# Gathers of adjacency rows moved from the column search to layer 0 of a four-layer graph network

## The chip, the cores and the metric

The program runs on one core of one Trainium2 chip. The metric is the device time of one execution in microseconds (us), median of several runs; smaller is better. An engine is called by its short name: PE (TensorE, matmuls), DVE (VectorE), ACT (ScalarE), POOL (GpSimd) and SP (SyncE, which here only issues DMAs). Each engine runs its own instructions in order and waits on semaphores for the others.

## What is computed

Four layers of a graph network on 2708 nodes with 512 features. The adjacency matrix `adj` (2708 x 2708, float32) is sparse, with a diagonal that is never zero; the low-numbered nodes have most of the edges. After each layer the result is added to the input and normalised over the features.

```python
# layer 0
adj_hat = adj + eye
d = 1 / sqrt(adj_hat.sum(axis=1))
x = layernorm(x + ((d[:, None] * adj_hat * d[None, :]) @ x) @ W.T + b)
# layer 1
head = (adj > 0) / max(sqrt(sum over the row of (adj > 0)), eps)
inc = adj + head
x = layernorm(x + (inc @ x) / inc.sum(axis=1))
# layer 2: attention over the edges, and a second sum with adj
x = layernorm(x + sigmoid(attn_a * x_a + attn_b * x_b))
# layer 3
x = layernorm(x + relu(adj @ ((x > 0) @ sign(weight).T)))
```

## The kernel before

The 2708 nodes are cut into 22 blocks of 128 rows (the last has 20). Block b of a layer's output needs only those columns of `adj` in which one of its rows has an entry. The kernel first finds these columns, then works with packed tiles alone: `packed[b]` holds, for block b, tiles of 128 found columns each (128 x 128 numbers, 64 KB). `ROOM[b]` is the number of such tiles, 9 for block 1 falling to 1 for block 21, 107 in all. Block 0, which has almost all columns, is not searched: it keeps whole column blocks in `packed[0]`. `DIRECT` names column blocks that a block loads whole instead of by index; those go over SP. `GROUPS` joins the blocks into nine groups: 1; 2, 3; 4 to 6; 7 to 9; 10 to 12; 13 to 15; 16 to 18; 19, 20; 21.

**The search** (inside `with in_order()`, L1128) takes one block per turn. SP loads the block's rows of `adj` (1.35 MB, two halves, four buffers), its rows of x and a tile for block 0, two turns ahead. DVE turns the rows into a 0/1 mask (L782, L784), PE counts with it which columns are hit (L801), and PE also transposes the block's x (L943) and multiplies it with the layer's weights (L958); ACT sums the rows (L733), keeps the transposed x (L950) and scales the product by `dinv`, which gives y (L967), written to the table `y_rows` in DRAM (L968). For each group, in the turns after its last block, DVE, PE and ACT turn the hits into a list of column numbers: `count` and `count_partitions` in the first turn, `steps_of` and `look_up` (L849, L870) in the second, `keep_looked` and `list_nodes` (L880, L890 to L910) in the third. `list_nodes` ends with `row_at`, the indices for the adjacency gathers, and puts each gather of the group into the list `to_fetch`. From the end of that turn on, `fetch` issues up to six of them in each turn on POOL (L928): an indirect DMA that takes 128 rows of the transposed matrix, 512 bytes of each, into one tile of `packed[b]`. `in_order` fixes the order on every engine as it is written, but POOL has no other work in the search, so its gathers run as soon as their indices are there. `own_diagonal` (L810) and `fold` (L979) are small DVE steps of each turn. `count_block0` and block 0's y (L967, last) end the stage.

**Layer 0** (loop at L1237) goes over the blocks in the order of `sequence`: 0, 1, 21, 2, 3, up to 20. For each block, POOL gathers rows of `y_rows` by the found column numbers (L570, 128 rows of 2 KB, 256 KB), `ROOM[b]` gathers per block into tiles with 10 buffers; a gather has to wait until PE has used the tile of ten gathers before. PE multiplies each with the packed tile (L1254), DVE adds and normalises (L1264, L615 to L631), SP writes the result to `x1_rows` (L1268). A first gather of `y_rows` can't start before all 22 blocks of y are written. Between the blocks stand steps of other kinds, keyed by the place in the sequence (`between`): loads and sums for later layers, and for each group `count_positive`, which counts positive entries in its packed tiles (L1017 on DVE, L1019 on PE), and `head_steps`, which turn these counts into layer 1's factors (`head_row`, `rdeg`, `own1`). Group n has its counts after place 2 + 2n and the rest after place 3 + 2n.

**Layer 1** gathers rows of `x1_rows`, so its first gather waits for the last block's write. Layers 1 to 3 read the packed tiles from SBUF again and gather features in the same way. A dense version of the whole network stands behind a test and isn't run with these inputs.

Of the kernel before, what the change touches and what calls it, by code (L numbers as in the profile page):

```python
# [12 lines left out]
I32 = mybir.dt.int32  # L13
# [6 lines left out]
P = 128  # L20
# [465 lines left out]
def sparse_layers(ctx, tc, x, adj, adj_t, w0_t, b0, w_sa, a_sa, w_gcnb, b_gcnb, wa, ba, wb, bb, w3_t,  # L486
# [10 lines left out]
    nc = tc.nc  # L497
    N, D = x.shape
    KC = D // P
    NB = -(-N // P)  # L500
# [6 lines left out]
    def direct(b: int):  # L507

        return tuple(range(NB)) if b == 0 else DIRECT.get(b, ())
# [49 lines left out]
    own1 = const.tile([P, NB], F32, name="s_own1")  # L559
    head0_row = const.tile([P, P], F32, name="s_head0_row")  # L560
    vl_row = const.tile([P, D], F32, name="s_vl_row")
    for t in (*f, f0_other):
        nc.vector.memset(t[:, D + 1 :], 0.0)

# [85 lines left out]
    with tc.tile_pool(name="s_pre", bufs=1) as pre:  # L650
# [232 lines left out]
        def list_nodes(g):  # L883
            b0_ = g[0]
            T = sum(ROOM[b] for b in g)
            look = search.pop(g)["look"]
            own = small.tile([P, TS], F32, tag="turns", name=f"turns{b0_}")
            at = 0
            for b in g:
                nc.vector.tensor_tensor(  # L890
                    own[:, at : at + ROOM[b]], order[:, : ROOM[b]],
                    look[:, at : at + ROOM[b], NB], op=ALU.subtract,
                )
                at += ROOM[b]
            nc.vector.tensor_tensor(own[:, :T], own[:, :T], look[:, :T, NB + 1], op=ALU.subtract)
            col = look[:, :T, :NB]
            nc.vector.tensor_tensor(
                col, col, own[:, :T, None].to_broadcast([P, T, NB]), op=ALU.is_equal
            )
            nc.vector.tensor_tensor(  # L900
                col, col, start[:, None, :].to_broadcast([P, T, NB]), op=ALU.mult
            )
            nc.vector.tensor_reduce(own[:, :T, None], col, axis=AX.X, op=ALU.add)
            nc.vector.scalar_tensor_tensor(
                index_of[b0_][:, :T], own[:, :T], float(PAD), look[:, :T, NB + 2],
                op0=ALU.add, op1=ALU.add,
            )

            row_at = small.tile([P, TS], I32, tag="row_at", name=f"row_at{b0_}")
            nc.vector.tensor_scalar(  # L910
                row_at[:, :T], index_of[b0_][:, :T], N - 1, None, op0=ALU.min
            )
            at = 0
            for b in g:
                m = rows(b)
                for i, j in enumerate(direct(b)):
                    nc.sync.dma_start(
                        packed[b][:, i, :], adj_t[j * P : (j + 1) * P, b * P : b * P + m]
                    )
                for t in range(ROOM[b]):  # L920
                    to_fetch.append((b, t, row_at[:, at + t : at + t + 1]))
                at += ROOM[b]

        to_fetch = []

        def fetch(n: int):
            for b, t, row in to_fetch[:n]:
                nc.gpsimd.indirect_dma_start(  # L928
                    out=packed[b][:, t + len(direct(b)), :], out_offset=None, in_=adj_t,
                    in_offset=bass.IndirectOffsetOnAxis(ap=row, axis=0), element_offset=b * P,  # L930
                )
            del to_fetch[:n]

        sum0 = ps_mm.tile([P, D], F32, tag="sum0", name="l0_0", bufs=1)
        summed = []
# [160 lines left out]
        def turn(at: int):  # L1096
            step_of = {at - last_at[g]: g for g in GROUPS}

            def chain(action, since: int):
                if since in step_of:  # L1100
                    action(step_of[since])

            each(degree, at - 1)
            each(root, at - 1)
            each(lambda b: b and own_diagonal(b), at - 1)
            each(sum_rows, at)
            each(lambda b: b and mark(b), at)
            each(load_x, at + 2)
            each(load, at + 2)
            each(transpose_x, at)  # L1110
            chain(steps_of, 2)
            chain(count, 1)
            each(scale0, at - 2)
            each(keep_transposed, at)
            each(project0, at - 1)
            chain(keep_looked, 3)
            chain(count_partitions, 1)
            chain(look_up, 2)
            each(inverse_root, at - 1)
            each(fold, at - 3)  # L1120
            each(grow0, at - 3)
            chain(list_nodes, 3)
            if to_fetch:
                fetch(6 if at < NTURN else len(to_fetch))
            if at == NTURN:
                count_block0()

# [30 lines left out]
    with tc.tile_pool(name="s_l0", bufs=10, reuse_waits="tile") as lp:  # L1158
# [62 lines left out]
        def several(*actions):  # L1221
            def act():
                for a in actions:
                    a()
            return act
# [4 lines left out]
        several(*others)()  # L1230
        for n, g in enumerate(GROUPS):
            steps_ = head_steps(g)
            between.setdefault(2 + 2 * n, []).append(
                several(lambda g=g: count_positive(g, lp), steps_[0])
            )
            between.setdefault(3 + 2 * n, []).append(several(*steps_[1:]))
        for at, b in enumerate(sequence):  # L1237
            m = rows(b)
            if b:
                src = [  # L1240
                    gathered(lp, D, y_rows, b, t) for t in range(ROOM[b])
                ]
                dsrc = []
                for i, j in enumerate(direct(b)):
                    if j == b:
                        own = lp.tile([P, D], F32, tag="own", name=f"y_own{b}", bufs=1)
                        nc.sync.dma_start(own[:m], y_rows[b * P : b * P + m, :])
                        dsrc.append(own)
                    else:
                        dsrc.append(first[0])  # L1250
                src = dsrc + src
                ps = ps_mm.tile([P, D], F32, tag="mm", name=f"l0_{b}")
                for i, moving in enumerate(src):
                    nc.tensor.matmul(  # L1254
                        ps[:m], packed[b][:, i, :], moving[:, :D],
                        start=(i == 0), stop=(i == len(src) - 1),
                    )
            else:
                ps = sum0
            if at > 1:  # L1260
                grow1(sequence[at - 2])
            t = work.tile([P, D], F32, tag="t", name=f"t0_{b}")
            old = place_of_x(b)
            nc.vector.scalar_tensor_tensor(  # L1264
                t[:m], ps[:m], dinv[:m, b : b + 1], old[:m, :D], op0=ALU.mult, op1=ALU.add
            )
            layernorm(old[:m, :D], t, m, f"0_{b}")
            nc.sync.dma_start(x1_rows[b * P : b * P + m, :], old[:m, :D])  # L1268
            for step_ in between.get(at, []):
                step_()  # L1270
        for b in sequence[-2:]:
            grow1(b)
    l0_ps.close()
# [550 lines left out]
```

## Time and profile before

| what | us |
|---|---|
| median of 3 runs | 1210.41 |
| lowest and highest run | 1210.06, 1212.56 |
| the profiled execution, its own time | 1219.48 |
| its span, first to last instruction | 1217.8 |

| stage of the profiled execution | from | to | length |
|---|---|---|---|
| search, up to the first gather of `y_rows` | 0 | 239.2 | 239.2 |
| layer 0, up to the first gather of `x1_rows` | 239.2 | 415.3 | 176.1 |
| layer 1 | 415.3 | 575 | 159.7 |
| layer 2 | 575 | 1062 | 487 |
| layer 3 | 1062 | 1217.8 | 155.8 |

| POOL's gathers by line | number | busy us | mean ns |
|---|---|---|---|
| L928, adjacency rows | 107 | 110.2 | 1030 |
| L570, rows of `y_rows` | 107 | 105.6 | 987 |
| L570, rows of `x1_rows` | 107 | 113.0 | 1056 |
| L1492, layer 2's rows | 107 | 106.1 | 991 |
| L570, rows of `xw_rows` | 83 | 82.9 | 998 |

How to read the views: a row of the timeline has the start, the duration, the engine, the line of the program, the operation, the tile written and the tiles read, how many rows are merged, and in square brackets the idle time of that engine before it and what ended that. "issue" there means that the engine waited for nothing that the profile shows, and "remote" that the semaphore's move can't be tied to an instruction. In a table of windows each engine has its busy time in the stretch, and the last three columns are the granted share of PE's full clock, the busy share of the DMA engines and what they moved. Ends of matmuls are modelled, so their rows are surer in their start.

### The profile page before, as it was taken

The numbers are of one execution on the slowest core, as the hardware profiler recorded it, in microseconds if no ns is written. First come the engines' busy times: TensorE is split into PE (matmuls) and PEld (weight loads), VectorE is DVE, ScalarE is ACT, GpSimd is POOL, SyncE is SP. The second block draws the span as 40 slices with busy tenths as digits, with TensorE's granted clock in tenths as the row PEclk, the third lists the DMA queues.
The fourth block names the chain that finished last, engine by engine and source line by source line (L and its number), as shares of the span: only waits on it lengthen the run. The fifth ranks groups of instructions, "written<-read, shape, count | busy, mean of one in ns | idle before, by whom it ended". The sixth has DMA issues, their size and how long they took to land. (4 is left out here: it accounts for less than half of the span.)

```text
span 1217.8 us, 13502 instructions
## 1 busy us (share of the span) xinstructions
PE 1007.9 (83%) x4009; PEld 608.2 (50%) x4028; DVE 726.2 (60%) x2556; ACT 403.4 (33%) x869; POOL 533.5 (44%) x545
## 2 busy tenths in 40 slices
PE   3865677579789789989799999999999999698852
PEld 2432333123334234445566677676666666476631
DVE  4764556464567676778656655656555554346765
ACT  4542444100000044668533223223232322243420
POOL 0455544676666377675332233222221211066660
PEclk9877778789799899999899999999999999889976
DMA  9875775476677677776332223223121211199982
GB/s 330 297 230 182 222 228 157 113 243 200 199 201 224 188 202 207 216 218 205 87 84 75 66 74 97 65 57 88 51 85 40 79 40 53 57 338 287 256 238 80
DMA packets 84523, 193.53 MB, mean 159 GB/s; under 512 B 13680, under 2 KB 26968, under 8 KB 84440
## 3 DMA queue, kind: packets, MB, share of 16 engines
q0 software_dynamic: 41056, 113.12, 33.8%
q1 hardware_dynamic: 31692, 64.45, 15.5%
q10 hardware_dynamic: 11692, 15.01, 3.8%
q8 instruction: 34, 0.56, 0.2%
q14 instruction: 49, 0.40, 0.1%
HBM read 155.73 MB, written 25.92 MB: 149 GB/s over the span
## 5 line engine op out<-in xcount | busy, mean ns | idle before, releaser
L1492 POOL DMA_INDIRECT xg<-x_rows,i x107 | 106.1, 991 | 216.9 <-DVE mv L619 63.3
L1337 PE MATMUL acc<-ae,xg 128*128 128x256 f32 x856 | 187.9, 378 | 0.4 <-ACT ae L1330 0.3
L1337 PEld LDWEIGHTS acc<-ae,xg 128*128 128x128 f32 x856 | 161.9, 190 | 23.0 <-ACT ae L1330 1.1
L928 POOL DMA_INDIRECT a<-in_adj_t_dram,row_at x107 | 110.2, 1030 | 128.6 <-DVE mask L782 83.6
L570 POOL DMA_INDIRECT xg<-x_rows,i x107 | 113.0, 1056 | 57.3 <-issue 26.2
L570 POOL DMA_INDIRECT xg<-y_rows,i x107 | 105.6, 987 | 53.3 <-issue 24.3
L1398 PE MATMUL l<-xg,inc 128*128 128x512 f32 x214 | 103.0, 617 | 15.6 <-DMA xg<-x_rows,i 12.4
L1254 PE MATMUL l<-xg,a 128*128 128x512 f32 x214 | 109.6, 645 | 7.6 <-issue 4.1
L570 POOL DMA_INDIRECT xg<-xw_rows,i x83 | 82.9, 998 | 46.1 <-issue 20.4
L958 PE MATMUL y<-s_w,xt 128*128 128x512 f32 (+1 forms) x176 | 96.1, 692 | 2.2 <-issue 2.0
L1534 PE MATMUL pg<-s_wg,pt 128*128 128x512 f32 (+1 forms) x176 | 82.7, 611 | 0.0
L1534 PE MATMUL ph<-s_wsa,pt 128*128 128x512 f32 (+1 forms) x176 | 79.3, 592 | 0.0
L621 POOL TENSOR_TENSOR rs<-mv,s_neg_half 128x1 f32<-128x1 f32 (+1 forms) x22 | 13.1, 596 | 150.8 <-DVE mv L619 150.5
L1398 PEld LDWEIGHTS l<-xg,inc 128*128 128x128 f32 x214 | 39.6, 194 | 72.2 <-issue 41.9
L1326 ACT ACTIVATE ae<-sl,xg 128x128 f32<-128x128 f32 x107 | 40.5, 394 | 99.8 <-DMA xg<-x_rows,i 88.6
L1337 PE MATMUL acc<-ae,f 128*128 128x256 f32 (+1 forms) x272 | 67.2, 390 | 7.4 <-ACT ae L1375 5.9
L1327 DVE SCALAR_TENSOR_TENSOR ae<-ae 128x128 f32<-128x128 f32 (+4 forms) x69 | 29.1, 422 | 66.8 <-ACT ae L1326 62.0
L1254 PEld LDWEIGHTS l<-xg,a 128*128 128x128 f32 x214 | 40.3, 202 | 56.7 <-issue 45.8
L1337 PEld LDWEIGHTS acc<-ae,f 128*128 128x128 f32 (+1 forms) x272 | 52.1, 195 | 25.3 <-issue 7.8
L958 PEld LDWEIGHTS y<-s_w,xt 128*128 128x128 f32 (+1 forms) x176 | 37.7, 227 | 50.7 <-issue 50.5
L615 DVE BATCH_NORM_STATS2 st<-t 128x6 f32<-128x512 f32 (+1 forms) x88 | 60.6, 689 | 1.2
L733 ACT ACTIVATE unused<-arow 128x1408 uint8<-128x1408 f32 (+3 forms) x44 | 58.3, 1326 | 0.9
(250 smaller groups left out, 1749.0 us busy)
## 6 DMA issues: line engine op xcount, KB each, us to landing
arow<-in_adj_dram SPq DMA_DIRECT2D x21, 704.0 KB
arow<-in_adj_dram SPq DMA_DIRECT2D x21, 650.0 KB
x_rows<-f SPq DMA_DIRECT2D x21, 258.0 KB
aw<-in_adj_t_dram SPq DMA_DIRECT2D x21, 256.0 KB
out_dram<-o SPq DMA_DIRECT2D x21, 256.0 KB
f<-in_x_dram SPq DMA_DIRECT2D x20, 256.0 KB
y_rows<-yt ACTq DMA_DIRECT2D x20, 256.0 KB
x_rows<-f SPq DMA_DIRECT2D x20, 256.0 KB
```

Source lines behind the costliest of these rows:

```text
L570: nc.gpsimd.indirect_dma_start(out=t[:, :dst_w], out_offset=None, in_=src[:, :], in_offset=bass.IndirectOffsetOnAxis(ap=index[b][:, i : i ...
L615: nc.vector.bn_stats(st[:m], t[:m])
L733: nc.scalar.activation(unused[:m, : ar.shape[1]], ar, AF.Copy, accum_out=row_sums[:m, b, h : h + 1])
L928: nc.gpsimd.indirect_dma_start(out=packed[b][:, t + len(direct(b)), :], out_offset=None, in_=adj_t, in_offset=bass.IndirectOffsetOnAxis(ap ...
L958: nc.tensor.matmul(ps[:m], xt[:, k, :m], w0[:, k, :], start=(k == 0), stop=(k == KC - 1))
L1254: nc.tensor.matmul(ps[:m], packed[b][:, i, :], moving[:, :D], start=(i == 0), stop=(i == len(src) - 1),)
L1326: nc.scalar.activation(ev[:, i, :], sl, AF.Identity, bias=score)
L1327: nc.vector.scalar_tensor_tensor(ev, ev, SLOPE, ev, op0=ALU.mult, op1=ALU.max)
L1337: nc.tensor.matmul(acc[:, k, :].rearrange("p (h i) -> p h i", h=2)[:, :, :m], src[:r, k * P : (k + 1) * P], ae[:r, :, :m], start=(is_first ...
L1398: nc.tensor.matmul(ps[:m], inc[:, i, :m], src[i0 + i][:, :D], start=(i0 + i == 0), stop=(i0 + i == len(src) - 1),)
L1492: nc.gpsimd.indirect_dma_start(out=g, out_offset=None, in_=x2_rows[:, :], in_offset=bass.IndirectOffsetOnAxis(ap=index[b][:, t : t + 1], a ...
L1534: nc.tensor.matmul(ps[:m], pt[:, k, h, :m], w[:, k, :], start=(k == 0), stop=(k == KC - 1))
```

## The change

The adjacency gathers leave the search. `list_nodes` still works out the indices, but into nine tiles that live through layer 0 (`row_at_of`, one for each group) in place of a tile that rotates over four buffers, and it appends nothing to `to_fetch`, which is gone with its `fetch`. Direct tiles are loaded by SP from `list_nodes` as before. In layer 0's loop a new `fetch(b)` issues all `ROOM[b]` adjacency gathers of the block just before the block's gathers of `y_rows`, held in program order. On POOL the order is so block 1's 9 and 9, block 21's 1 and 1, block 2's 8 and 8, and so on to block 20's 4 and 4. Since a group's packed tiles are now complete only when its last block's turn comes, the counts of positive entries follow the group's last place in the sequence (`behind`), and the remaining head steps the place after it; the last group's (blocks 19 and 20) fall after the loop.

```diff
+    row_at_of = {
+        g: const.tile([P, sum(ROOM[b] for b in g)], I32, tag=f"r{g[0]}", name=f"r{g[0]}")
+        for g in GROUPS
+    }
...
-            row_at = small.tile([P, TS], I32, tag="row_at", name=f"row_at{b0_}")
+            row_at = row_at_of[g]
             nc.vector.tensor_scalar(
                 row_at[:, :T], index_of[b0_][:, :T], N - 1, None, op0=ALU.min
             )
...
-                for t in range(ROOM[b]):
-                    to_fetch.append((b, t, row_at[:, at + t : at + t + 1]))
-                at += ROOM[b]
-
-        to_fetch = []
-
-        def fetch(n: int):
-            for b, t, row in to_fetch[:n]:
-                nc.gpsimd.indirect_dma_start(
-                    out=packed[b][:, t + len(direct(b)), :], out_offset=None, in_=adj_t,
-                    in_offset=bass.IndirectOffsetOnAxis(ap=row, axis=0), element_offset=b * P,
-                )
-            del to_fetch[:n]
...
-            if to_fetch:
-                fetch(6 if at < NTURN else len(to_fetch))
...
         for n, g in enumerate(GROUPS):
             steps_ = head_steps(g)
-            between.setdefault(2 + 2 * n, []).append(
+            behind = max(sequence.index(b) for b in g)
+            between.setdefault(behind, []).append(
                 several(lambda g=g: count_positive(g, lp), steps_[0])
             )
-            between.setdefault(3 + 2 * n, []).append(several(*steps_[1:]))
+            between.setdefault(behind + 1, []).append(several(*steps_[1:]))
+
+        def fetch(b: int):
+
+            for t in range(ROOM[b]):
+                row = row_at_of[group_of[b]]
+                at = at_of[b] + t
+                i = nc.gpsimd.indirect_dma_start(
+                    out=packed[b][:, t + len(direct(b)), :], out_offset=None, in_=adj_t,
+                    in_offset=bass.IndirectOffsetOnAxis(ap=row[:, at : at + 1], axis=0),
+                    element_offset=b * P,
+                )
+                tc.keep_in_program_order(i)
+
         for at, b in enumerate(sequence):
             m = rows(b)
             if b:
+                fetch(b)
                 src = [
                     gathered(lp, D, y_rows, b, t) for t in range(ROOM[b])
                 ]
...
+        for step_ in between.get(NB, []):
+            step_()
         for b in sequence[-2:]:
             grow1(b)
```

## The prediction

> **What bounds the kernel now.** I read the page, then the busy time by stage, then GpSimd's (POOL's) instructions in order of time, then the timeline of one disturbed stretch of the search. Times are us from the span's start. The first view gives the stages: the search with the projection (0 to 239.2, where the first gather of `y_rows` starts), layer 0 (to 415.3, where the first gather of `x1_rows` starts), layer 1.
>
> ```profile
> core 0: us, PE busy (x) PEld busy (x) DVE busy (x) ACT busy (x) POOL busy (x), PEclk, DMA share, GB/s
> 0.00:239.20 239.20, 155.95 (x908) 78.69 (x908) 135.03 (x590) 96.78 (x175) 111.37 (x118) 0.83 0.68 218
> 239.20:415.30 176.10, 145.63 (x431) 60.24 (x430) 106.48 (x447) 12.12 (x45) 107.03 (x108) 0.91 0.68 206
> 415.30:575.00 159.70, 142.27 (x380) 71.40 (x381) 116.65 (x408) 91.01 (x150) 113.02 (x107) 0.96 0.75 217
> ```
>
> In layer 0 PE is busy 145.6 of 176.1: PE bounds it, with POOL (107.0 busy) close behind. In the search no engine is busy two thirds of the time. The page has what a gather costs POOL:
>
> ```profile
> L928 POOL DMA_INDIRECT a<-in_adj_t_dram,row_at x107 | 110.2, 1030 | 128.6 <-DVE mask L782 83.6
> L570 POOL DMA_INDIRECT xg<-y_rows,i x107 | 105.6, 987 | 53.3 <-issue 24.3
> ```
>
> POOL's own timeline shows the rhythm, one every 1.25 (0.95 busy, 0.30 between) when nothing is waited for, and the edges of the stages:
>
> ```profile
> 108.68 1.29 POOL L928 DMA_INDIRECT a<-in_adj_t_dram,row_at  x1 [0.30 <-issue]
> 110.28 0.95 POOL L928 DMA_INDIRECT a<-in_adj_t_dram,row_at  x1 [0.30 <-issue]
> 122.51 1.54 POOL L928 DMA_INDIRECT a<-in_adj_t_dram,row_at  x1 [11.29 <-DVE mask L782]
> ...
> 236.28 0.95 POOL L928 DMA_INDIRECT a<-in_adj_t_dram,row_at  x1 [0.30 <-issue]
> 239.24 0.95 POOL L570 DMA_INDIRECT xg<-y_rows,i  x1 [2.02 <-issue]
> ...
> 400.06 0.95 POOL L570 DMA_INDIRECT xg<-y_rows,i  x1 [0.30 <-issue]
> 415.31 0.95 POOL L570 DMA_INDIRECT xg<-x_rows,i  x1 [14.31 <-DMA s_bab<-in_ba_dram]
> ```
>
> Why is the search so empty? In its timeline the other engines stand still while POOL runs a burst of adjacency gathers (86.2 to 111.2), and go on as the burst ends:
>
> ```profile
> 98.25 0.15 DVE L741 SCALAR_TENSOR_TENSOR deg<-s_row_sums 128x1 f32<-128x1 f32 x1
> 108.13 0.16 DVE L810 SCALAR_TENSOR_TENSOR s_dia_own<-find,s_dia 128x1 f32<-128x1 f32 x1 [9.73 <-remote]
> 113.77 0.59 ACT L950 COPY xt<-pt 128x512 f32<-128x512 f32 x1 [18.67 <-remote]
> 114.53 0.58 PE L870 MATMUL looked<-steps,after 128*128 128x25 bf16 x16 [14.50 <-ACT steps L858]
> ```
>
> The reader should see that L810 waits for the L801 matmuls and L950 for the L943 transposes, whose rows end at 96.0 and 96.5; the semaphore records of the trace move PE's counter only at 108.1 and 113.7. This recurs with each of the six long bursts: the last gather starts at 74.4, 110.3, 142.4, 173.2, 199.8 and 236.3, and the waiting L950 goes on at 76.1, 113.8, 145.9, 176.7 and 203.0, and in the sixth block 0's L967 at 234.9. Between bursts no such delay occurs. DMA is not full then: 43 GB/s at 108 to 112.
>
> **What the Trainium skill says.** "DMA: Bandwidth & Descriptors", section "SWDGE vs HWDGE vs iDMA": descriptors of gathers are computed in software on GpSimd's cores and written to rings in SBUF. The trace agrees with a price per instruction rather than per byte: 0.95 for 64 KB (adjacency) as for 256 KB (features). "SBUF — State Buffer", section "SBUF: two separate sides": GpSimd and a VectorE operation in a two-port mode lock each other out. The trace has single gathers up to 2.06 in the search against a median of 0.947, a mean excess of 0.08; the delay of PE's semaphore by 12 and 17 us it does not explain, nor does any page I know of. "TensorE: Matmul & The Clock Gate", section "What's actually happening": PE's clock halves when PE has been idle and comes back after about 3.4 us of work; the trace grants 0.50 in the standing stretch 104 to 112.
>
> **The change part by part.** *Added to layer 0.* POOL's order of the changed kernel is 9 adjacency gathers of block 1, its 9 of features, 1 and 1 of block 21, 8 and 8 of block 2, and so on, strictly alternating. The first 9 still run in the search, since their indices exist at 37. Everything after the first feature gather is in line: 107 + 98 = 205 gathers. At layer 0's mean 0.987 + 0.30 = 1.287 that is 263.8, against 160.8 now (239.24 to 400.06): **+103**. At the undisturbed 1.25 it is 256.3, +95. Only 160.8 - 107 x 1.287 = 23.1 of the present stretch is POOL waiting, so at most this could have hidden any of it: POOL becomes the bound. PE's 145.6 then fits inside; at half clock it would come near 265 (x 0.91 / 0.5), but it warms when busy, so no cost is put there.
>
> *POOL's own waits.* The feature tiles have 10 buffers, so a feature gather needs PE's matmul of ten gathers before. Ten now stand some 20 gathers (25 us) apart, so PE itself is never late, but its semaphore may be, as in the search. Bounds: 0 if it arrives within 25 us; 45 if POOL stops 4 us (longest stop for PE in layer 0: 3.6) in each of some 11 rounds of the buffers. I take **+15**, less than the 23.1 of now.
>
> *End of layer 0.* From the last gather's start to layer 1's first gather is 15.25, in which PE works off a backlog of two blocks (8 x 2 records of 3.6 to 3.7 us each). Without backlog: landing 3.3 (the chain of waits has 3.3 for such a gather in layer 2), a matmul 0.9, the block's DVE and ACT chain 3.7 (408.6 to 412.4), the write and its landing 2.9, and a gather's 1.25: about 12. **-3**, bounds -4 and 0. The head counts, now tied to the end of each group, leave those of blocks 19 and 20 after the loop; they run on DVE beside the 2.9 of the write and block 1's landing gathers, so nothing; uncovered about 4.
>
> *Removed from the search.* 98 gathers, 6.4 MB and their bursts. POOL itself isn't on the path to 239.24: that waits for `y_rows` of block 0 (issued 235.6). What goes is the standing. Starts of the mask memset L782 mark the turns: the turns after each list take 5.5 to 6.5, the next ones, in the burst, 13.2, 16.7, 17.2, 15.8 and 12.9 (sum 75.8), the third ones 11.9, 14.1, 8.5 and 8.2 (sum 42.7; they carry the list and refill loads the standing held up). Undisturbed I put 7 for five seconds (35) and 8 for four thirds (32): -40.8 and -10.7. The last block's L967 waits 12.5 for a matmul group ended at 222.5: -12. Together -63.5; I take **-62**. Bounds: -72 if every second turn takes 6 and every third 7, -40 if a third of the standing has another cause. PE's work (155.95 over 22 turns, 7.1 each at clock 0.83) forbids much more. What is late next there is PE, with the adjacency loads.
>
> *Indices.* Nine persistent index tiles in place of a rotating buffer: same DVE instructions, nothing. SP loses nothing: loads of direct tiles stay in the search.
>
> Sum: -62 + 103 + 15 - 3 = **+53**. The profiled execution took 1219.48 (span 1217.8), so about 1272 beside it; the median of runs without a profile is 1210.41, 9 less, and gives **1263**.
>
> **The rivals.**
> (a) *The standing stays*: the bursts and the late semaphores only coincide, say because turn and burst have the same period. For: no page or queue explains the link. Against: six long bursts out of six, each wait ending between 1.4 before and 3.5 after the last gather's start. The search gains 5: -5 + 103 + 15 - 3 = +110, **1320**.
> (b) *Late semaphores move along*: POOL is now busy without rest, and PE, DVE and ACT hear of each other only when it stops. For: in layer 0 the records of PE's counter already stand up to 6.6 behind its matmuls. Then POOL's waits cost 45: -62 + 103 + 45 - 3 = +83, **1293**.
> (c) *The other side*: with POOL silent, the search falls to what PE and DMA need, and gains all that layer 0 loses. It decides from a gain of 100, that is, the first feature gather by 139. PE's 155.95 at full clock is 129, so with no POOL waits and 1.25 per gather: -110 + 95 + 0 - 4 = -19, **1191**. Against: turns free of bursts take 5.5 to 8, and the first 55 us stay as they are: 55 + 14 turns x 6.5 + 22 of tail (204.3 to 239.2 less 12.5) = 168.
> (d) *Nothing moves* because a scheduler hoists the gathers back: excluded by the order of instructions, which alternates.
>
> **How the numbers follow.** The forecast has 0.66, (b) 0.15, (a) 0.13, (c) 0.04, others 0.02. Low end: -72 + 95 + 0 - 4 = +19, 1229. High: (b) lies inside, (a) at the edge; -40 + 103 + 45 - 3 = +105, 1316. About what this kernel's runs can tell from no change is 0.2% (2.4 us): faster 0.03, same 0.02, slower 0.95.
>
> **What would show it.** Right: first `y_rows` gather near 177, none of L810's and L950's waits above 5 us in the search after 55, POOL's gaps in layer 0 at 0.30 with waits of 15 in sum, PE's share in layer 0 near a half, first `x1_rows` gather near 468, later stages as before. Wrong: the standing still there without bursts (a), long POOL waits for PE in layer 0 (b), a first feature gather before 140 (c).

## The result, and the profile after

Times are in us, here and below.

| | before | after |
|---|---|---|
| median of 3 runs | 1210.41 | 1282.57 (1280.59 to 1284.81) |
| ratio | | 1.0592, interval 1.0558 to 1.0625 |
| the profiled execution, its own time | 1219.48 | 1284.81 |
| its span | 1217.8 | 1283.1 |
| search, up to the first gather of `y_rows` | 239.2 | 166.6 |
| first to last gather of `y_rows` | 160.8 | 295.7 |
| last gather of `y_rows` to first of `x1_rows` | 15.2 | 23.2 |
| the rest (layers 1 to 3) | 802.5 | 797.6 |

The change costs 5.9 per cent. In the profiled executions the search gains 72.6, the row of gathers in layer 0 loses 134.9, the end of layer 0 loses 8.0 and the later layers gain 4.9: +65.4. The medians are 72.2 apart, because the profiled execution of before lay 9 over its median and that of after only 2.

The busy time by stage of the changed kernel (the stretches are the search, layer 0, layer 1):

```profile
core 0: us, PE busy (x) PEld busy (x) DVE busy (x) ACT busy (x) POOL busy (x), PEclk, DMA share, GB/s
0.00:166.60 166.60, 137.55 (x908) 70.54 (x908) 130.85 (x584) 96.87 (x174) 12.91 (x21) 0.96 0.83 275
166.60:485.50 318.90, 163.41 (x431) 66.52 (x430) 108.67 (x455) 12.54 (x46) 197.39 (x205) 0.73 0.47 134
485.50:641.60 156.10, 140.44 (x368) 69.15 (x368) 114.10 (x395) 87.67 (x145) 108.72 (x107) 0.95 0.74 218
```

In the search PE's instructions are the same 908, but they take 137.6 where they took 156.0: the granted clock rose from 0.83 to 0.96, now that PE no longer stands (137.6 x 0.96 and 156.0 x 0.83 are 132 and 129, nearly the same). In layer 0 PE's share falls from 145.6 of 176.1 to 163.4 of 318.9, and POOL is the one that is busy: 197.4, and 0.30 between one gather and the next. The two groups of gathers:

```profile
L574 POOL DMA_INDIRECT xg<-y_rows,i x107 | 103.3, 966 | 186.0 <-DVE hd L1028 116.6
L1233 POOL DMA_INDIRECT a<-in_adj_t_dram,r x107 | 104.5, 976 | 66.3 <-DVE mask L786 34.0
```

The price of one has not changed (0.97, before 0.99 and 1.03); the number in layer 0 has. POOL's timeline at the edges of the stages:

```profile
166.61 1.11 POOL L574 DMA_INDIRECT xg<-y_rows,i  x1 [116.61 <-DVE hd L1028]
...
462.29 0.95 POOL L574 DMA_INDIRECT xg<-y_rows,i  x1 [0.30 <-remote]
485.52 0.94 POOL L574 DMA_INDIRECT xg<-x_rows,i  x1 [22.28 <-DMA s_bab<-in_ba_dram]
```

POOL is silent for 116.6 of the search, and in this time no engine waits for a late semaphore. ACT's waits from 50 to 166.6, first of the kernel before (there to 239), then of after; the columns are what was waited for, the sum, how often, the longest:

```profile
ACT xt L950 <- remote: 53.5, 6, 18.7
```

```profile
ACT root L756 <- DVE deg L745: 25.8, 16, 3.0
ACT xt L941 <- PE pt L934: 5.6, 4, 4.0
```

L950 of before is L941 of after. Its six waits (3.8 to 18.7), whose end could not be tied to an instruction, are gone; what is left is the wait for the transposes themselves. In layer 0 such waits are there instead (all engines, 166.6 to 485.5):

```profile
DVE t L1268 <- remote: 85.5, 7, 20.7
ACT s_head_row L1062 <- remote: 78.9, 4, 47.2
...
PEld L1010 <- DVE pos L1008: 40.1, 5, 21.9
```

These engines have time to spare in layer 0. POOL hasn't, and it waits as well:

```profile
POOL xg L574 <- PE l L1258: 24.5, 14, 9.8
...
POOL xg L574 <- remote: 13.7, 9, 3.3
POOL xg L574 <- PE hr L1010: 4.1, 1, 4.1
POOL xg L574 <- PE l L1198: 2.8, 2, 2.5
```

Together 45 in 26 waits, each with the usual 0.30 in it: 37 of true waiting. Worked out from the other side: 205 gathers keep POOL busy for 196.4 up to the last one's start (197.4 less 0.95), 204 gaps of 0.30 make 61.2, and 295.7 less these 257.6 leaves 38 of waiting.

### The profile page after: what moved, and what is told of

It is laid out like the page before. It is cut to its first block, busy times and chain, and to the rows that moved or that the text cites. A ratio compares the mean times of both kernels' runs of the same rounds, so it can differ in the third digit from the quotient of the medians.

```text
span 1283.1 us, 13592 instructions
## 1 busy us (share of the span) xinstructions
PE 1007.6 (79%) x4009; PEld 606.5 (47%) x4028; DVE 724.2 (56%) x2556; ACT 404.4 (32%) x869; POOL 522.0 (41%) x545
## 5 line engine op out<-in xcount | busy, mean ns | idle before, releaser
L1498 POOL DMA_INDIRECT xg<-x_rows,i x107 | 106.2, 992 | 216.5 <-issue 65.2
L574 POOL DMA_INDIRECT xg<-y_rows,i x107 | 103.3, 966 | 186.0 <-DVE hd L1028 116.6
L574 POOL DMA_INDIRECT xg<-x_rows,i x107 | 109.1, 1020 | 69.6 <-issue 26.6
L1258 PE MATMUL l<-xg,a 128*128 128x512 f32 x214 | 120.8, 713 | 14.0 <-DMA xg<-y_rows,i 12.8
L1233 POOL DMA_INDIRECT a<-in_adj_t_dram,r x107 | 104.5, 976 | 66.3 <-DVE mask L786 34.0
L1404 PE MATMUL l<-xg,inc 128*128 128x512 f32 x214 | 103.4, 623 | 10.6 <-DMA xg<-x_rows,i 7.3
L574 POOL DMA_INDIRECT xg<-xw_rows,i x83 | 83.4, 1005 | 45.2 <-issue 19.4
L949 PE MATMUL y<-s_w,xt 128*128 128x512 f32 (+1 forms) x176 | 88.8, 652 | 0.0
L1268 DVE SCALAR_TENSOR_TENSOR t<-l,s_dinv,f 128x512 f32<-128x512 f32 (+1 forms) x21 | 15.7, 749 | 121.9 <-remote 85.5
L1258 PEld LDWEIGHTS l<-xg,a 128*128 128x128 f32 x214 | 46.2, 228 | 78.1 <-issue 50.9
L603 ACT ACTIVATE rsqs<-mv 128x1 f32<-128x1 f32 (+1 forms) x66 | 13.4, 202 | 191.8 <-DVE mv L623 67.9
```

The lines of the kernel that those rows point to most:

```text
L574: nc.gpsimd.indirect_dma_start(out=t[:, :dst_w], out_offset=None, in_=src[:, :], in_offset=bass.IndirectOffsetOnAxis(ap=index[b][:, i : i ...
L949: nc.tensor.matmul(ps[:m], xt[:, k, :m], w0[:, k, :], start=(k == 0), stop=(k == KC - 1))
L1233: i = nc.gpsimd.indirect_dma_start(out=packed[b][:, t + len(direct(b)), :], out_offset=None, in_=adj_t, in_offset=bass.IndirectOffsetOnAxi ...
L1258: nc.tensor.matmul(ps[:m], packed[b][:, i, :], moving[:, :D], start=(i == 0), stop=(i == len(src) - 1),)
L1404: nc.tensor.matmul(ps[:m], inc[:, i, :m], src[i0 + i][:, :D], start=(i0 + i == 0), stop=(i0 + i == len(src) - 1),)
L1498: nc.gpsimd.indirect_dma_start(out=g, out_offset=None, in_=x2_rows[:, :], in_offset=bass.IndirectOffsetOnAxis(ap=index[b][:, t : t + 1], a ...
```

## The experiments

There were twelve runs in four groups. A group runs on one chip, with runs of the kernel before beside it; another group may have another chip, and this turned out to matter most. The first and third groups were on chips whose kernel before takes 1210 and 1215, like the one above; the second and fourth on chips where it takes 1109. Times of different groups are not compared without the kernel before beside them. As far as is known, each chip was used by one group only. What is put down to a chip below may therefore belong to its state at that time. On the two faster chips the kernel before has times but no trace.

| run | time | before there | ratio, interval | last turn starts | first, last `y_rows` | first `x1_rows` |
|---|---|---|---|---|---|---|
| (before) | 1210.4 | | | 204.3 | 239.2, 400.1 | 415.3 |
| (after) | 1282.6 | 1210.4 | 1.0592, 1.0558 to 1.0625 | 145.7 | 166.6, 462.3 | 485.5 |
| e1_both | 1366.6 | 1210.4 | 1.1269, 1.1192 to 1.1347 | 190.0 | 231.0, 543.0 | 563.5 |
| e2_pool_busy | 1335.7 | 1210.4 | 1.0997, 1.0931 to 1.1063 | 160.7 | 200.8, 511.9 | 533.2 |
| e3_plain_loads | 1169.8 | 1210.4 | 0.964, 0.9585 to 0.9694 | 172.2 | 195.1, 354.4 | 369.2 |
| e4_gated | 1213.8 | 1210.4 | 1.0007, 0.9974 to 1.004 | 193.7 | 226.8, 392.7 | 406.8 |
| e5_half | 1146.4 | 1109.5 | 1.033, 1.0284 to 1.0375 | 143.0 | 164.0, 360.9 | 373.1 |
| e6_half_spaced | 1189.1 | 1109.5 | 1.0714, 1.0675 to 1.0753 | 150.8 | 206.2, 401.2 | 413.9 |
| e7_last21 | 1113.6 | 1109.5 | 1.0033, 1.0018 to 1.0047 | 143.4 | 164.9, 329.2 | 342.0 |
| e8_bufs16 | 1206.1 | 1109.5 | 1.087, 1.0836 to 1.0904 | 140.9 | 161.4, 420.1 | 432.5 |
| e9_after_again | 1285.7 | 1215.0 | 1.0612, 1.0522 to 1.0702 | 145.4 | 166.4, 458.5 | 478.8 |
| e10_bufs16_again | 1290.6 | 1215.0 | 1.0649, 1.0559 to 1.0738 | 146.0 | 166.6, 458.4 | 487.9 |
| e11_half_spaced_again | 1187.2 | 1109.0 | 1.0729, 1.0685 to 1.0772 | 148.5 | 203.4, 399.0 | 411.5 |
| e12_last21_again | 1112.9 | 1109.0 | 1.0034, 1.0021 to 1.0047 | 143.2 | 164.3, 328.4 | 341.4 |

The start of the last turn (its mask memset) tells what the search's engines need; the first gather of `y_rows` also waits for whatever POOL or SP still have to do before it.

### Gathers in both places

`e1_both` puts the gathers back in the search and leaves them in layer 0 too:

```diff
@@ list_nodes(g), changed kernel
+                for t in range(ROOM[b]):
+                    to_fetch.append((b, t, row_at[:, at + t : at + t + 1]))
...
@@ turn(at), changed kernel
             chain(list_nodes, 3)
+            if to_fetch:
+                fetch_early(6 if at < NTURN else len(to_fetch))
```

> The changed kernel with the 107 adjacency gathers issued in the search as well, as the kernel before has them (same places, same order), and again in layer 0: the search of one kernel with the layer 0 of the other. Theory (dense gathers on POOL hold back the semaphores of PE, DVE and ACT, and that is why the search stood): the first feature gather starts near 239 again and not at 167, the turns under a burst take 13 to 17 again; layer 0 as in the changed kernel, plus up to 11 for block 1's 9 adjacency gathers, which now queue behind the search's bursts. 1282.6 + 72 + 0 to 11 = 1355 to 1366. Rival (bursts and late semaphores only coincide, the search got shorter for another reason): 1283 to 1294.

It took 1366.6, at the upper end of the theory's 1355 to 1366. The first feature gather is back from 166.6 to 231.0, and the last turn starts at 190.0 and not at 145.7. ACT's waits from 50 to 166.6 are those of the kernel before again, where the changed kernel has none (L954 is L950 of before):

```profile
ACT xt L954 <- remote: 38.5, 6, 12.1
```

With the kernel before, after and this one, three of the four combinations of "gathers in the search" and "gathers in layer 0" are there, and the two costs add: 64 to 73 for the search (231.0 or 239.2 against 166.6), and 143 for layer 0 (134.9 and 8.0 at its end), or 156 in `e1_both`, which has block 1's nine gathers in line as well. That bursts and standing only coincide is ruled out on this chip.

The 64 are not all standing. The last y that the feature gathers need, block 0's, is sent off at 218.1 (changed kernel 163.2, kernel before 235.6), and the first feature gather then still stands behind the rest of POOL's burst. So these bursts held the search up by 55 in this execution and by 72 in that of the kernel before.

### A busy POOL without gathers, and the bytes without POOL

`e2_pool_busy` is `e1_both` with the gather replaced:

```diff
@@ fetch_early(n)
-                nc.gpsimd.indirect_dma_start(
-                    out=packed[b][:, t + len(direct(b)), :], out_offset=None, in_=adj_t,
-                    in_offset=bass.IndirectOffsetOnAxis(ap=row, axis=0), element_offset=b * P,
-                )
+                nc.gpsimd.tensor_copy(busy[:, 0:1], row)
+                nc.gpsimd.iota(busy, pattern=[[1, ROOM[1] * P]], base=0, channel_multiplier=0)
```

> As e1_both, but each of the 107 gathers in the search is replaced by work on POOL that moves nothing by DMA: a copy of the index column (so that it starts when the gather could) and an iota of 1152 numbers (1.09 in the kernel before). POOL is as busy as with the bursts. Theory (it is the gather, its descriptors or its traffic, that holds the semaphores back): the search stays near 167, 1283 to 1294. Rival (a busy POOL by itself holds the others back): search near 239, 1355 to 1366.

`e3_plain_loads` is the kernel before with this edit:

```diff
@@ fetch(n), kernel before
-                nc.gpsimd.indirect_dma_start(
-                    out=packed[b][:, t + len(direct(b)), :], out_offset=None, in_=adj_t,
-                    in_offset=bass.IndirectOffsetOnAxis(ap=row, axis=0), element_offset=b * P,
-                )
+                nc.sync.dma_start(
+                    packed[b][:, t + len(direct(b)), :],
+                    adj_t[(t + 3) * P : (t + 4) * P, b * P : b * P + m],
+                )
```

> The kernel before with each adjacency gather replaced by a plain load of the same 64 KB shape on SP's queue, of 128 consecutive rows instead of the listed ones, in the same places of the program (the output is then that of other adjacency columns). There are no adjacency gathers anywhere, the bytes are the same. Theory (the work of POOL's gathers is what holds semaphores back, not their traffic): search near 167, layer 0 about 161 from first to last feature gather, 1210 - 72 = about 1138. Rival (the traffic of the 6.4 MB is what the search waited for): search near 239, about 1210.

By their times both fell between the two theories (1335.7 and 1169.8), so the traces have to decide. In `e2_pool_busy` POOL works without a pause:

```profile
119.58 1.09 POOL L934 IOTA a<- 128x1152 int32 x1
120.73 0.28 POOL L933 COPY a<-r 128x1 int32<-128x1 int32 x1
121.08 1.09 POOL L934 IOTA a<- 128x1152 int32 x1
```

and ACT's waits from 50 to 166.6 are those of the changed kernel, with no late semaphore:

```profile
ACT root L756 <- DVE deg L745: 33.9, 15, 3.0
ACT xt L953 <- PE pt L946: 7.3, 7, 1.8
ACT xt L953 <- PE find L853: 6.5, 5, 1.4
```

Its last turn starts at 160.7, 15 later than without this work and 29 earlier than with gathers. The first feature gather comes as late as 200.8 only because POOL's own filler, 1.5 per item, lasts until then: the expectation had not counted this. So the theory holds, with up to 15 left for a busy POOL as such. The trace has a likely cause for these: DVE's own instructions take longer beside the copies and iotas. The same two, first in the changed kernel, then here:

```profile
75.64 0.83 DVE L788 TENSOR_SCALAR mask<-arow 128x1300 bf16<-128x1300 f32 x1
76.97 0.17 DVE L829 COPY s_found<-turn 128x3 f32<-128x3 f32 x1
```

```profile
78.36 1.43 DVE L788 TENSOR_SCALAR mask<-arow 128x1300 bf16<-128x1300 f32 x1
80.28 0.72 DVE L829 COPY s_found<-turn 128x3 f32<-128x3 f32 x1
```

In all DVE is busy 170 in this search (641 instructions) and 140 in that of `e1_both` (620). No run tests whether this is the whole of the 15.

`e3_plain_loads` leaves the indices out and loads consecutive rows, so it is a test and no candidate. There are no late semaphores in its search either. What its engines wait for (all engines, 50 to 195.1) is data:

```profile
DVE mask L784 <- DMA arow<-in_adj_dram: 33.0, 25, 5.0
...
ACT unused L733 <- DMA arow<-in_adj_dram: 26.7, 22, 4.9
```

The 107 loads stand on SP's queue before the rows of later blocks, which then come late; 24 of them are issued only after the last turn has begun. So the bytes cost something, but by another road. Layer 0, with no adjacency gathers, takes 159.3 from first to last feature gather, as before.

The semaphore records of the traces say the same. Counted are the instructions that raise an engine's counter, from 50 to 160, and whose raise is recorded over 2 late (the longest in brackets), and, over the whole span, PE's raising instructions and the records of PE's counter:

| run | PE | DVE | ACT | PE's instructions, records |
|---|---|---|---|---|
| before | 14 (12.1) | 19 (8.1) | 13 (19.9) | 785, 665 |
| after | 0 | 0 | 0 | 785, 673 |
| e1_both | 20 (11.1) | 26 (12.1) | 15 (13.8) | 789, 666 |
| e2_pool_busy | 0 | 0 | 0 | 789, 670 |
| e3_plain_loads | 0 | 0 | 0 | 785, 670 |
| e4_gated | 19 (11.4) | 16 (9.9) | 12 (14.5) | 786, 660 |
| e5_half | 0 | 0 | 0 | 776, 778 |
| e7_last21 | 1 (3.4) | 0 | 0 | 776, 775 |
| e12_last21_again | 1 (3.5) | 0 | 0 | 776, 776 |

In the first six rows there are fewer records than instructions, as if several raises came in as one (the layers behind the search have gathers in every run). From 50 to 160 alone, DVE's raising instructions and records are 180 and 108 in before, 184 and 105 in `e1_both` and 213 and 133 in `e4_gated`, but 294 and 294 in after, 249 and 249 in `e2_pool_busy` and 213 and 213 in `e3_plain_loads`: in these six runs records are missing in the search only where gathers run. The Trainium skill, "Perfetto Trace Analysis", section "Tensor Engine Instruction (MATMUL, LD_WEIGHTS)", has the semaphore update pushed when PSUM has acknowledged the write, and then a propagation. The last three rows agree, with none or one over 2; in before, `e1_both` and `e4_gated` it comes up to 12 after the matmul's modelled end, and there the measurement decides.

### Shorter bursts

`e4_gated` releases at most five gathers in a turn, through a small copy of their indices by DVE at the end of the turn:

```diff
@@ fetch(n), kernel before
+            gate = small.tile([P, 8], I32, tag="gate", name=f"gate{now[0][0]}_{now[0][1]}", bufs=4)
...
+                    nc.vector.tensor_copy(
+                        gate[:, k : k + same], rows_of(b)[:, t : t + same]
+                    )
...
-            if to_fetch:
-                fetch(6 if at < NTURN else len(to_fetch))
+            fetch(PACE)
```

> The kernel before with the gathers of adjacency released at most five in a turn, by a copy of their index columns on DVE at the end of each turn; before, all of a list's 13 to 18 went as soon as the list was there. All 107 stay in the search. Theory in its first form (the semaphores come through whenever POOL pauses, so many short bursts disturb less than a few long ones): the turns are even, none above 12, search between 190 and 215, 1160 to 1185. Rival (each gather in the search costs about 72 / 98 = 0.7 us, however they are spread): search near 239, 1205 to 1215.

The rival was right: 1213.8, no different from before. The first feature gather starts at 226.8, but eight adjacency gathers still follow it and the second feature gather comes at 239.4, near the rival's 239. Block 0's y is sent off at 217.3, as late as in `e1_both`. The first form of the theory fell, at least as this kernel tests it. Part of the reason may be the gate: bursts of 5 often join, as POOL's timeline shows after 83.4:

```profile
83.35 1.48 POOL L948 DMA_INDIRECT a<-in_adj_t_dram,gate  x1 [6.86 <-DVE mask L788]
85.14 1.17 POOL L948 DMA_INDIRECT a<-in_adj_t_dram,gate  x1 [0.30 <-issue]
...
103.14 1.19 POOL L948 DMA_INDIRECT a<-in_adj_t_dram,gate  x1 [0.30 <-issue]
111.13 1.60 POOL L948 DMA_INDIRECT a<-in_adj_t_dram,gate  x1 [6.79 <-DVE mask L788]
```

ACT's waits for late semaphores still come to 44.2 in six.

### A part of the gathers, spread out, or with more tiles: on another chip

`e5_half`, `e6_half_spaced` and `e7_last21` share the first part of the edit; the number is 10, 10 and 16. `e6_half_spaced` has the second part as well. `e8_bufs16` is the changed kernel with the third part alone.

```diff
+EARLY = range(1, 10)
...
-                for t in range(ROOM[b]):
+                for t in range(ROOM[b] if b in EARLY else 0):
                     to_fetch.append((b, t, row_at[:, at + t : at + t + 1]))
...
-                fetch(b)
+                if b not in EARLY:
+                    fetch(b)
@@ e6_half_spaced: fetch_early(n), after each gather
+                for _ in range(2):
+                    nc.gpsimd.iota(
+                        space, pattern=[[1, ROOM[10] * P]], base=0, channel_multiplier=0
+                    )
@@ e8_bufs16
-    with tc.tile_pool(name="s_l0", bufs=10, reuse_waits="tile") as lp:
+    with tc.tile_pool(name="s_l0", bufs=16, reuse_waits="tile") as lp:
```

> The changed kernel with the adjacency gathers of blocks 1 to 9 (59) back in the search, in bursts as before, and those of the other blocks (48) in layer 0. Theory: each gather brought back costs the search 72.6 / 98 = 0.74 of standing: 50 x 0.74 = 37 (first feature gather near 204). Layer 0: 155 gathers x 1.287 = 199.5 and 15 to 20 of POOL's waits, 55 to 60 over the kernel before, and 5 at the end. 1210 - 35 + 57 + 5 = 1237, between 1225 and 1247. If only long bursts harm and the first lists' bursts do nothing: about 1205.

> As e5_half, but after each of the 59 gathers in the search POOL fills some 1.3 with two iotas into a tile that layer 0 overwrites later, so that the gathers come one in 2.5 and not one in 1.25. Theory with density (only back-to-back gathers hold the semaphores back): the turns take 6 to 8 like those of the changed kernel, first feature gather between 167 and 180, 1198 to 1215. Rival (each gather costs the search 0.74 however far apart): as e5_half, 1225 to 1247.

> As e5_half, but blocks 1 to 15 (86 gathers) in the search and only blocks 16 to 21 (21 gathers, those of the last lists) in layer 0, about as many as POOL's 23 of waiting there could take. Theory: the search gains 21 x 0.74 = 16 and up to 9 more because its last burst, which the last block waits for, is gone; layer 0 has 128 gathers x 1.287 = 165 and 15 to 20 of waits, 20 to 25 more than before. 1200 to 1216, the same as before within what can be told. A clear gain (under 1195) would say that the waiting of POOL in layer 0 can take the gathers in.

> The changed kernel with 16 feature tiles in layer 0 in place of 10, so that POOL may run some 12 gathers (15) further ahead of PE. Theory (POOL loses its 36 of waits because PE's semaphore comes later than the 25 that ten tiles allow): waits fall to about 10, last feature gather 15 to 26 earlier, 1257 to 1268. Rival (the semaphores come only when POOL stops, so POOL runs on until it must stop, whatever the tiles): fewer but longer stops of the same sum, 1275 to 1287.

On this chip the kernel before took 1109.5, 101 less, and none of these times can be read against the expectations as they stand. The reason is in the search of `e7_last21`. POOL gathers there back to back, 86 of them:

```profile
79.44 0.94 POOL L933 DMA_INDIRECT a<-in_adj_t_dram,r  x1 [0.30 <-issue]
80.69 0.94 POOL L933 DMA_INDIRECT a<-in_adj_t_dram,r  x1 [0.30 <-issue]
81.94 0.95 POOL L933 DMA_INDIRECT a<-in_adj_t_dram,r  x1 [0.30 <-issue]
```

and ACT, which stood for up to 19 at a time under such a burst on the other chips, goes on beside it, L955 with waits of 1.4 at most (timeline, then the waits of 50 to 164.9):

```profile
75.74 0.58 ACT L955 COPY xt<-pt 128x512 f32<-128x512 f32 x1 [0.43 <-PE pt L948]
82.30 0.58 ACT L955 COPY xt<-pt 128x512 f32<-128x512 f32 x1 [1.32 <-PE find L854]
88.29 0.58 ACT L955 COPY xt<-pt 128x512 f32<-128x512 f32 x1 [0.40 <-PE pt L948]
```

```profile
ACT root L757 <- DVE deg L746: 26.2, 15, 3.0
ACT xt L955 <- PE find L854: 5.6, 4, 1.4
```

The search with 86 dense gathers takes 164.9, with 9 of them (`e8_bufs16`) 161.4. The theory's 0.74 per gather is worth nothing here: the standing needs a chip of the other kind as well as the dense gathers.

What does remain is the price on POOL. `e8_bufs16` by stages (search, layer 0):

```profile
0.00:161.41 161.41, 133.54 (x908) 69.59 (x908) 130.47 (x584) 96.90 (x174) 13.20 (x22) 0.97 0.84 284
161.41:432.49 271.08, 183.18 (x432) 66.07 (x430) 107.62 (x455) 12.55 (x46) 197.44 (x205) 0.81 0.56 158
```

POOL's 197.4 for 205 gathers is that of the changed kernel to 0.1, but from first to last feature gather it takes 258.7 and not 295.7: nearly all of the 38 of waiting is gone (258.7 - 196.5 - 61.2 = 1), and the end takes 12.4. The Trainium skill, "DMA: Bandwidth & Descriptors", section "SWDGE vs HWDGE vs iDMA", with its descriptors made in software, fits this: a fixed price per gather of 0.96 and 0.30, alike on both chips and for 64 and 256 KB. With nothing to gain in the search, this kernel is 8.7 per cent slower than before there.

`e5_half` follows the same arithmetic: 155 gathers in 196.9 (1.27 each), 36 more than the kernel before has on the other chip. `e6_half_spaced` has its POOL fillers until 206; they cost the search itself 8 (150.8 against 143.0) and hold the first feature gather by 42.

### The changed kernel and the 16 tiles once more

> The changed kernel itself, unaltered. The first group of runs was on a chip whose kernel before takes 1210, the second on one where it takes 1109 and no engine waits for a semaphore that comes late, dense gathers or not. Theory (the late semaphores belong to the chip, the price of a gather on POOL to the kernel): on a chip like the second there is no standing to gain: the search ends near 162 with or without the gathers, layer 0 takes 205 x 1.26 = 258 between first and last feature gather and not 160, and the change costs all of the 98: 1109 + 95 to 100 = 1204 to 1212, ratio 1.086 to 1.093. On a chip like the first: 1275 to 1290, ratio 1.055 to 1.063. Rival (the kernel with its 10 tiles waits for PE on the second chip too, as it does on the first): on the second 1220 or more.

> The changed kernel with 16 feature tiles, as e8_bufs16, here beside e9_after_again on one chip, so that the two tell what the six tiles are worth there. On a chip like the second: nothing, within 5 of e9_after_again, since POOL waits for nothing. On a chip with late semaphores, theory (the six tiles outlast the delays): 15 to 26 less than e9_after_again. Rival (POOL runs on until it must stop, and the stops are as long in sum): within 7 of it.

This group came to a chip with late semaphores. The changed kernel took 1285.7 and 1.0612 of before, as on the first. Beside it the 16 tiles are worth nothing (1290.6), which the rival had said: both take 292 from first to last feature gather. POOL's waits of `e10_bufs16_again` (166 to 486) are as long in sum as those above:

```profile
POOL xg L574 <- remote: 23.4, 12, 4.3
POOL xg L574 <- PE l L1258: 14.2, 8, 5.4
```

Against 1 of waiting on the other chip with the same program. So the waits are not there because ten tiles are too few. What happens instead may be that POOL takes up what tiles there are and then has to stop, and that the semaphores come in only then; that is argued, not shown. The end of layer 0 is longer with the 16 tiles, 29.5 against 20.3.

### What was left

> The kernel of e6_half_spaced, meant for a chip with late semaphores (on one without it takes 1189: POOL's fillers last until 206 and hold the first feature gather, while the last turn starts at 151). The measure is the turns: with dense gathers the turns that start at 77, 101 and 119 (e1_both) or 74, 91 and 108 (the kernel before) are the ones drawn out, and the last starts at 190 to 204; without gathers it starts at 146. Theory with density (one gather in 2.7 lets the semaphores through): no turn between 60 and 150 above 9, the last starts by 160, first feature gather 206 to 212. Rival (each gather costs its 0.74 however far apart): turns of 12 and more, the last starts at 146 + 50 x 0.74 = 183 or later.

> The kernel of e7_last21 (blocks 16 to 21, 21 gathers, in layer 0; the other 86 in the search), meant for a chip with late semaphores; on one without it takes 1114 against 1109 of the kernel before. Theory, as for e7_last21: the search loses the standing of the last bursts, 16 to 25, layer 0 takes 20 to 25 more, 1200 to 1216 where the kernel before takes 1210 to 1215. Under 1195 would make it the better one there.

Both were meant for a chip with late semaphores and came to one without (before 1109.0). They repeat `e6_half_spaced` and `e7_last21` to 0.2 per cent, on a second chip of this kind. Whether gathers at one in 2.7 would let the semaphores through, and what the last 21 are worth on a chip with late semaphores, stays open. Of the versions that gather the listed rows, none beat the kernel before on the chips where it ran: `e4_gated` equals it on one with late semaphores, `e7_last21` is 0.3 per cent slower on the two without.

## Why the prediction was right

The sign and the bound held: +72 where +53 was said, inside the range, and POOL bounds layer 0 as worked out. The nearness of the total is in part luck. On the profiled executions POOL's waits cost 23 more than was put and the end of layer 0 costs 11 more, while the search gained 10.6 more, the gathers cost 6 less and the later layers, put at nothing, gained 4.9. By its steps:

- **Search, -62.** It gained 72.6, the bound given. The first feature gather came at 166.6 and not near 177. But the 72.6 hangs on one execution of the kernel before, which lies 9 over its median; against `e1_both` the gain is 64 to the first feature gather and 55 to block 0's y, so the 62 is within what executions differ by. The second turns after a list took 5.8 to 7.3 (7 was said), the thirds 7.5 to 8.0 (8 was said). The starts of the turns gained 58.6 up to the last (204.3 to 145.7), where the sum had 51.5, and what follows the last turn gained 14.1 (35.0 to 20.9), where it had 12: the turns that the sum left out, the first and the last ones, had stood a little too. That the gathers caused the standing on this chip is shown by `e1_both`; that it is the gather and neither a busy POOL nor only its bytes, by `e2_pool_busy` and `e3_plain_loads`. Which part of a gather's work does it isn't shown.
- **205 gathers in line, +103.** 257.6 against 160.8: +97. The mean of 0.987 was a little high; 0.96 was measured. The 257.6 is the one figure that both kinds of chip share (257.7 in `e8_bufs16`).
- **POOL's own waits, +15.** This term was mis-sized: 38, close to the 45 of rival (b). That late semaphores would make POOL wait was right: on a chip without them it is 1 (with 16 tiles). The way it was to come about, one semaphore outlasting the 25 that ten tiles cover, is not what the runs show: as far as the records tell, PE's raises in layer 0 are up to 18.8 late, less than 25, and six tiles more changed nothing. PE had waited for DVE as well (11.8 below), so the delays of several engines may add up; this stays open. The choice of 15, "less than the 23.1 of now", reasoned from a layer 0 in which POOL paused often and PE's raises were up to 6.6 late.
- **End of layer 0, -3.** It was +8: 23.2 in place of 15.2. The estimate of 12 assumed that no backlog is left. But with late semaphores DVE and PE are behind when POOL stops. The last rows before the first gather of `x1_rows` begin so, on DVE and on PE:

```profile
464.30 0.75 DVE L1268 SCALAR_TENSOR_TENSOR t<-l,s_dinv,f 128x512 f32<-128x512 f32 x1 [10.26 <-remote]
```

```profile
466.99 0.19 PE L1010 MATMUL hr<-s_ones_b,pos 128*128 128x1 bf16 x1 [11.77 <-DVE pos L1008]
...
469.15 5.01 PE L1258 MATMUL l<-xg,a 128*128 128x512 f32 x6
475.28 3.68 PE L1258 MATMUL l<-xg,a 128*128 128x512 f32 x8
```

PE has stood for 11.8 and then works off the last blocks, though the last gather started at 462.3. Where nothing is late the end takes 12.2 to 13.0 (the six runs of the second and fourth groups), which was the estimate.

The first gather of `x1_rows` came at 485.5, where 468 was said; PE's share of layer 0 is 0.51, near the half that was said.

Of the rivals, (a) is refuted by the search of after and by `e1_both`. (b), that the late semaphores move along, is what happened in layer 0; its total of 1293 was too high by 10. The prediction weighed it at 0.15 as if it were another case; it was a part of the likeliest one. (c) would have needed 100 out of the search; it gave 73.

What the prediction could not see from one trace is that the -62 has no hold on other chips. There the cost in layer 0 stands alone: with 16 tiles the time is 1206.1 against 1109.5, 97 more, or 1.087. The changed kernel itself was not run on such a chip.

## What to carry to other kernels

Price a moved gather by what POOL pays for it, per instruction, and first look in which stage POOL has that time left: here 98 gathers cost 97 to 135 in a stage that POOL was about to bound. In one where it idled they had cost 55 to 73 on a chip with late semaphores, and next to nothing on the two without (the search took 164.9 and 164.3 with 86 gathers, 161.4 with 9). When engines stand for no reason that the program gives, look at when the semaphores were raised against when the instructions ended, and run the kernel before on a second chip before building on a cure. Here the delay that one engine's dense work caused went with this work when it was moved; it did not stay behind in the old stage.

## What the runs showed of the hardware that was not expected

- On two of the chips (and that of the first measurements) back-to-back indirect gathers on POOL hold back the raises of PE's, DVE's and ACT's semaphores, by up to 12, 12 and 20 in the search, and fewer are then recorded than there are instructions (665 records for 785). On two other chips the same instructions at the same distance of 1.25 do nothing of the kind (775 for 776), and the same kernel is faster by 101 of 1210. Why the chips differ, and whether one keeps to its kind at another time, isn't known.
- These 101 are not the search alone. From the first gather of `x1_rows` to the end, `e8_bufs16` takes 768.9 and `e7_last21` 767.9 where before and after take 802.5 and 797.6: some 30 in the later layers.
- An iota and a copy on POOL without a pause don't delay a semaphore: none over 2 in `e2_pool_busy` between 50 and 160. They do lengthen some instructions of DVE: between 55 and 140, L829 takes 0.85 in the mean where it takes 0.17 beside a silent POOL and 0.31 beside gathers (`e1_both`), and L788 takes 1.18 where it takes 0.83 and 0.86.
